# Attention output on TensorE: 64 matmuls of 32 rows and 32 columns a batch, or 40 of two shapes

## The chip, the cores and the metric

The kernel runs on one core of a Trainium2 chip. The metric is device time in microseconds (us) of one execution. The time before is 591.05 us, the median of three runs (589.9, 591.05 and 591.2).

## What is computed

A graph attention layer over 16 batches of 512 rows with 512 features, in fp32. Cut to what matters here:

```python
self_feat = concat([v, q], -1) @ W_self.T + b_self          # 16 x 512 x 512
output = self_feat
for d in range(2):                                          # both directions of the adjacency
    kv = self_feat[:, :20]                                  # 20 rows are keys and values
    aff = einsum('bnhd,bmhd->bnhm', qh, kh) / sqrt(32)      # 16 heads of 32
    w = softmax(where(mask, aff, NEG) + label_bias, -1)     # 20 weights a row, head, direction
    out_t = einsum('bnhm,bmf->bnhf', w, kv)
    output += einsum('bnhf,hgf->bnhg', out_t, Wout[d]) + bout[d]
return v + relu(output)
```

For each row and head there are 40 softmax weights, 20 of each direction. The kernel multiplies `kv` by `Wout` once, ahead of the loop, so that the attention output of a head is one product: its 40 weights by 40 value rows of 32 columns.

## The kernel before

**Setup** (to about 92 us): values, keys and bias terms of all batches are computed with small matmuls and written to DRAM. Line 544, 594, 658 and 683 are its matmuls; those of `keys` (L683) take 32 rows of the array and all 128 columns ("32\*128" in the profile's rows), those of L594 and L658 128 rows and 32 columns.

**Main loop**: 16 batches `b`, four tiles `nt` of 128 rows each. The instruction order is written out by hand, in program order for each engine. For a tile, TensorE computes `scores` (L357, 128 rows by 64 columns of the array, 32 records a tile); VectorE adds mask and bias terms, takes the maximum and subtracts it (`weigh`, L370, L374, L378); ScalarE takes the exponential (L383); in the next tile's step VectorE sums (L409) and takes the reciprocal (L410), GpSimd multiplies (`normal`, L411), and VectorE turns the weights (`turn`, L418). Between the scores TensorE computes the next batch's `self_feat` by seven half-size products (`product`, L284), which VectorE collects (`partial` L291, `joined` L301).

**The weights' place.** After `weigh` the partitions of a tile hold two head halves of 64 rows each; along a partition lie two row halves `g`, 8 heads, 2 directions and 20 weights: 640 numbers. `turn` is one VectorE transpose of 128x640, which turns each 32x32 block by itself. Afterwards a quarter `q` of the partitions holds 32 consecutive weights in its 32 rows, and 32 rows of the batch along the partition. As a head has 40 weights and a block 32, a head's weights lie in two neighbouring blocks.

**The values' place.** `blocks` (L152, 12 DMAs) writes the value rows to a DRAM tensor `bd_d`, after `clear_blocks` (L145) has filled all its 2 MB with zeros: for each head two blocks of 32 rows and 32 columns, the value rows at the places where the head's weights lie in the two blocks, and zeros elsewhere. `load_values` (L136, four DMAs a batch) loads a batch's blocks. All of these are issued from SyncE's queue (SP).

**The attention output.** `attend` (L420) runs over two column halves `c`, the two blocks `i`, four heads `e` and four quarters `q`: 64 matmuls, each 32 rows by 32 columns of the array, over 256 columns of moving data (4 tiles, 2 row halves, 32 rows). Quarter `q` picks the array's rows and the PSUM bank, `e` its columns; so 16 consecutive matmuls use 16 different parts of the array. Block `i=0` starts a sum in PSUM and `i=1` ends it. Each fp32 matmul is two passes, and each pass has a weight load of its own: a matmul leaves two load and two matmul records, 128 of each a batch. `attend(b - 1)` stands in tile `nt == 2` of batch `b`, after the scores of tile 1 and before those of tile 2; `finish` (L442) then adds `self_feat` on VectorE. The last batch is different: its scores, softmax, `turn_half` (L402, transposes of 128x320) and two calls of `attend` (three tiles, then one) stand at the end of the kernel, with `put_self` (L790) ahead of each.

Of the kernel before, what the change touches and what calls it, by code (L numbers as in the profile page):

```python
# [7 lines left out]
F32 = mybir.dt.float32  # L8
# [5 lines left out]
P = 128  # L14
# [4 lines left out]
def gat_kernel(  # L19
# [20 lines left out]
    nc = tc.nc  # L40
    B, F, N = xT.shape
    NG, L = adj.shape[3], adj.shape[4]
    H, DH = 16, 32
    C = F // P
    HL = P // DH
    NT = N // P
    BM = B * NG
    S = 2 * NG
    W = H * S
# [3 lines left out]
    HA = 2  # L53
    RA = P // HA
    HH = H // HA
    WA = WD // HA
    HN = (N - NG) // 2
    SCALE = float(1.0 / DH**0.5)

    PSUM = bass.MemoryType.PSUM  # L60
    DRAM = bass.MemoryType.DRAM
    const = ctx.enter_context(tc.tile_pool(name="const", bufs=1))
    dram = ctx.enter_context(tc.tile_pool(name="dram", bufs=1, space=DRAM))
# [6 lines left out]
    def bank(name, at=None):  # L70

        tag = {} if at is None else {"bufs": 1}
        return acc["pool"].tile([P, 512], F32, tag="acc" if at is None else f"acc{at}", name=name, **tag)
# [8 lines left out]
    bb_sb = const.tile([P, 1], F32, name="bb_sb")  # L82
    kvn = const.tile([P, C, BM], F32, name="kvn")
    g0 = const.tile([P, C, WD], F32, name="g0")
    zero = const.tile([P, HL * 2 * DH], F32, name="zero")

    cq_d = dram.tile([B, H, 2, NG], F32, name="cq_d")
    vw_d = dram.tile([2, C, BM, P], F32, name="vw_d")
    bd_d = dram.tile([C, B, 32, HL, 2, DH], F32, name="bd_d")
    g_d = dram.tile([C * C, P, B - 2, WD // C], F32, name="g_d")  # L90
    g1_d = dram.tile([C * C, P, WD // C], F32, name="g1_d")
    nz_d = dram.tile([B, N], F32, name="nz_d")
# [1 line left out]
    xs, xns, rss, adjs, nzs, sfs, cqs, gs, vds = {}, {}, {}, {}, {}, {}, {}, {}, {}  # L94
    adds, fulls, wts, outs, held, sf_ps, conds, prods = {}, {}, {}, [], [None] * 3, {}, {}, {}
# [39 lines left out]

    def load_values(b):  # L136

        vds[b] = gp.tile([P, HA, HL, 2, DH], F32, tag="vd", name=f"vd{b}", bufs=1)
        for q in range(HL):
            nc.sync.dma_start(  # L140
                vds[b][bass.ts(q, 32)].rearrange("p c e i g -> p c (e i g)"),
                bd_d[bass.ts(q // HA, HA), b].rearrange("c r e i g -> r c (e i g)"),
            )

    def clear_blocks(zero):  # L145

        nc.sync.dma_start(
            bd_d.rearrange("c b r e i g -> (c b r) (e i g)").rearrange("(n p) w -> p n w", p=P),
            zero.unsqueeze(1).to_broadcast([P, C * B * 32 // P, HL * 2 * DH]),
        )  # L150

    def blocks():  # L152

        bb = bd_d.rearrange("c b r e i g -> (c b) r e i g")
        vv = vw_d.rearrange("d c (b m) (e g) -> d (c b) m e g", m=NG, e=HL)
        for e in range(HL):
            for i in range(2):
                j = (e * S) // 32 + i
                for d in range(2):
                    lo = max(e * S + d * NG, 32 * j)  # L160
                    hi = min(e * S + (d + 1) * NG, 32 * j + 32)
                    if lo < hi:
                        m, r = lo - e * S - d * NG, lo - 32 * j
                        nc.sync.dma_start(bb[:, r : r + hi - lo, e, i], vv[d, :, m : m + hi - lo, e])


    def row_sum(b, j):
# [66 lines left out]
    def half(l):  # L234
        return slice(NG + l * HN, NG + (l + 1) * HN)

# [3 lines left out]
    def x_sum(b, n):  # L240

        t = sums[b, n] = xsum.tile([P, 2, HN], F32, tag=f"t{n}", name=f"t{b}_{n}")
        one, two = {
# [7 lines left out]
    def product(b, n):  # L251
# [17 lines left out]
        for i in range(2):  # L269
            for k in range(2):  # L270
                for a in range(HA):
# [5 lines left out]
                    if n in (2, 3, 5):  # L277
                        to = parts[b, "d" if n == 2 else "c"][bass.ts(a, RA), bass.ts(i, HN)]
                        start = k == 0 if n == 2 else (n, i, k) == (5, 0, 0)
                        stop = k == 1 if n == 2 else (n, i, k) == (3, 1, 1)  # L280
                    else:
                        to = parts[b, "a"][i][bass.ts(a, RA), :HN]
                        start, stop = (n, k) == (1, 0), (n, k) == (4, 1)
                    nc.tensor.matmul(to, lhs, x[:, k], start=start, stop=stop, skip_group_check=n != 2)  # L284

    def partial(b, n, f, l, to=None):

        if to is None:
            to = us[b, n] = xsum.tile([P, 2, HN], F32, tag=f"u{n}", name=f"u{b}_{n}")
        for i in range(2):  # L290
            done["partial"] = nc.vector.scalar_tensor_tensor(  # L291
                to[:, i], nzs[b][:, half(l)], qw[:, 2 * f + i, b : b + 1], parts[b, "a"][i][:, :HN],
                ALU.mult, ALU.add,
            )
# [72 lines left out]
    def weigh(b, nt, ps, between=None):  # L367

        f = softmax_view(fulls.pop((b, nt)))
        nc.vector.tensor_add(  # L370
            f[:, :, :, 1:], ps[:, :, :WA].rearrange("p g (h m) -> p g h m", m=ND), f[:, :, :, 1:]
        )
        mx = ps[:, 0, WA : WA + 2 * H].rearrange("p (g h) -> p g h", g=2)
        nc.vector.tensor_reduce(mx, f, AX.X, ALU.max)  # L374
        if between is not None:
            between()
        s = soft.tile(full, F32, tag="s", name=f"s{b}_{nt}", bufs=3)
        nc.vector.tensor_sub(s, f, mx.unsqueeze(3).to_broadcast(full))  # L378
        return s
# [16 lines left out]
    def normal_half(b, nt, s, a, engine):  # L396
# [2 lines left out]
        nc.vector.reciprocal(sm, sm)  # L399
        engine.tensor_mul(s[:, a], s[:, a], sm.unsqueeze(2).to_broadcast([P, H, NG]))  # L400

    def turn_half(b, nt, s, a):  # L402
        nc.vector.transpose(
            wts[b][:, nt, bass.ts(a, W // 2)], s[:, a].rearrange("p h m -> p (h m)")
        )

    def normal(b, nt, s):
        sm = soft.tile([P, 2, H], F32, tag="sm", name=f"sm{b}_{nt}")
# [4 lines left out]
    def turn(b, nt, s):  # L413


        if nt == 0:
            wts[b] = work.tile([P, NT, W], F32, tag="wt", name=f"wt{b}")
        nc.vector.transpose(wts[b][:, nt], s.rearrange("p a h m -> p (a h m)"))  # L418

    def attend(b, banks, tiles=slice(0, NT), start=True, stop=True):  # L420


        wt = wts[b][:, tiles].rearrange("p t (g w) -> p (t g) w", g=HA)
        w = wt.shape[1] * 32
        for c in range(HA):
            for i in range(2):
                for e in range(HL):
                    j = (c * HL + e) * S // 32 + i
                    for q in range(HL):
                        r = bass.ts(q, 32)  # L430
                        nc.tensor.matmul(  # L431
                            banks[q][bass.ts(e, DH), bass.ts(c, w)].rearrange("p (t n) -> p t n", n=32),
                            vds[b][r, c, e, i], wt[r, :, bass.ts(j, 32)],
                            start=start and i == 0, stop=stop and i == 1, skip_group_check=True,
                        )

    def turned(t, q, c=slice(0, HA), lo=0, hi=NT):

# [25 lines left out]
    with tc.tile_pool(name="setup", bufs=1) as sp, tc.tile_pool(name="ps_acc", bufs=4, space=PSUM) as acc["pool"]:  # L464
# [18 lines left out]
        with tc.tile_pool(name="setup_k", bufs=1) as sk:  # L483
# [81 lines left out]
            for c in range(C):  # L565
                nc.tensor.matmul(
                    ps[:, c % 2, c // 2 * B : (c // 2 + 1) * B], q4[:, bass.ts(c, P)], sel,
                    start=True, stop=True,
# [55 lines left out]
        with tc.tile_pool(name="setup_g", bufs=4) as sg:  # L624
# [49 lines left out]
            def keys(runs):  # L674
# [14 lines left out]
                for fc, hg, d, lo, hi in runs:  # L689
# [51 lines left out]
            first = None  # L741
            for n, runs in enumerate(bursts):
# [34 lines left out]
    gp = ctx.enter_context(tc.tile_pool(name="gp", bufs=2))  # L777
# [5 lines left out]
    with tc.manual_schedule():  # L783
# [13 lines left out]
        banks = None  # L797
        for b in range(B):
# [7 lines left out]
            for nt in range(NT):  # L806
# [20 lines left out]
                s = None  # L827

                if nt == 0:
# [41 lines left out]
                if nt == 1:  # L871
# [17 lines left out]
                    s = weigh(b, nt, pair)  # L889
# [10 lines left out]
                if nt == 2:  # L900
# [4 lines left out]
                    if b > 0:  # L905
                        banks = [bank(f"ps_o{b - 1}_{q}", q) for q in range(4)]
# [12 lines left out]
                    s = weigh(b, nt, pair, (lambda: partial(b + 1, 1, 0, 0)) if more else None)  # L919
# [10 lines left out]
                if nt == 3 and more:  # L930
# [18 lines left out]
                    s = weigh(b, nt, pair, lambda: partial(b + 1, 3, 1, 1))  # L949
# [9 lines left out]
                if final:  # L959
# [10 lines left out]
                    s = soft.tile(full, F32, tag="s", name=f"s{b}_{nt}", bufs=3)  # L970
# [11 lines left out]
        b = B - 1  # L982
# [23 lines left out]
        for q in (2, 3):  # L1006
            w = (NT - 1) * P
# [58 lines left out]
```

## Time and profile before

| | |
|---|---|
| runs | 589.9, 591.05, 591.2 us |
| the profiled execution | 591.14 us, of which 589.4 us are the span from the first to the last instruction |
| granted TensorE clock | 0.998 |
| TensorE matmul busy | 581.0 us (99%) |
| VectorE busy | 493.6 us (84%) |
| GpSimd busy | 382.6 us (65%) |
| ScalarE busy | 296.4 us (50%) |
| `attend`, matmuls of 256 columns, 15 batches | 41.4 us |

How to read it: a row of instructions gives the line of the kernel, the engine, the operation, the tile written and the tile read, the shapes, a count, and busy time and mean duration of one, or in views by time the start and the length in us. PE is TensorE's matmul, PEld its weight load, DVE VectorE, ACT ScalarE, POOL GpSimd, SP SyncE. "32\*32" in a matmul's row is the number of rows and columns of the array that it uses. Rows that touch are merged with a count; "<-" names what ended an idle time.

### The profile page before, as it was taken

How to read it: one execution, taken by the hardware profiler on the slowest of the kernel's cores; microseconds unless marked ns; L12 is line 12 of the kernel's file. 1: busy time of each engine (PE TensorE's matmuls, PEld its weight loads, DVE VectorE, ACT ScalarE, POOL GpSimd, SP SyncE). 2: the span in 40 equal slices, each digit the busy share in tenths (PEclk: the TensorE clock that was granted, in tenths of full speed). 3: DMA queues.
4: the chain of work that ended last, by engine and by line, in shares of the span. 5: the costliest groups of instructions: out<-in, count | busy, mean ns of one | idle time of the engine just before them, and what ended most of it. 6: DMA issues, size and time to landing. Idle time of an engine off the chain costs nothing.

```text
span 589.4 us, 17257 instructions
## 1 busy us (share of the span) xinstructions
PE 581.0 (99%) x7004; PEld 357.1 (61%) x7004; DVE 493.6 (84%) x785; ACT 296.4 (50%) x778; POOL 382.6 (65%) x351
## 2 busy tenths in 40 slices
PE   8999999999999999999999999999999999999996
PEld 4444447886666666666565656566666666666655
DVE  0496565889898989999898989898989898989896
ACT  1234442546464655556464646464747464646441
POOL 2225663648677675858585868685858586776774
PEclk9999999999999999999999999999999999999999
DMA  8999999966758495858675757666675757482504
GB/s 291 351 389 352 340 377 324 274 167 192 221 144 249 149 249 159 246 136 245 159 230 174 212 170 211 197 183 204 183 218 174 221 165 232 142 246 83 175 20 145
DMA packets 99615, 126.70 MB, mean 215 GB/s; under 512 B 19441, under 2 KB 71697, under 8 KB 97489
## 3 DMA queue, kind: packets, MB, share of 16 engines
q1 hardware_dynamic: 98288, 123.72, 68.3%
q0 software_dynamic: 672, 1.36, 1.0%
q8 instruction: 55, 0.90, 0.6%
q10 hardware_dynamic: 576, 0.53, 0.3%
q14 instruction: 24, 0.19, 0.1%
HBM read 85.71 MB, written 40.24 MB: 214 GB/s over the span
## 4 chain that ended last, share of the span: by engine, by line
PE 95%; DVE 2%; DMA 2%; ACT 0%; POOL 0%; SPq 0%; issue 0%; DVEq 0%; POOLq 0%; ACTq 0%
PE ps_s L357 44%; PE ps_a L284 17%; PE ps_c L284 8%; PE ps_o L431 7%; PE ps_d L284 4%; PE ps_v L658 3%; PE ps_k L594 3%; PE ps_sf L207 2%; DMA ws_q<-in_wsT 2%; PE ps_kv L544 1%; PE ps_nz L191 0%; POOL s L411 0%; PE ps_c L630 0%; PE ps_q L554 0%; PE ps_g(0, 2, 0, 1, 2)0_487 L683 0%
## 5 line engine op out<-in xcount | busy, mean ns | idle before, releaser
L357 PE MATMUL ps_s<-g,sf 128*64 128x304 f32 x2048 | 273.6, 420 | 0.5 <-ACT st L698 0.5
L357 PEld LDWEIGHTS ps_s<-g,sf 128*64 128x64 f32 x2048 | 152.2, 137 | 107.3 <-issue 6.2
L411 POOL TENSOR_TENSOR s<-s,sm 128x640 f32<-128x640 f32 x63 | 80.1, 1272 | 128.8 <-DVE sm L410 128.8
L383 ACT ACTIVATE s<-s 128x640 f32<-128x640 f32 x63 | 46.5, 738 | 167.4 <-DVE s L378 167.4
L319 ACT ACTIVATE prod<-adj,wb_sb 128x80 f32<-128x80 int32 x330 | 111.6, 427 | 0.0
L347 POOL TENSOR_TENSOR full<-cq,both 128x640 f32<-128x640 f32 x64 | 99.4, 1553 | 3.1 <-ACT both L338 1.5
L370 DVE TENSOR_TENSOR full<-ps_s,full 128x608 f32<-128x608 f32 x63 | 49.8, 791 | 36.1 <-PE ps_s L357 30.8
L455 POOL TENSOR_TENSOR o<-o,x 128x512 f32<-128x512 f32 x60 | 75.4, 1276 | 0.0
L338 ACT COPY both<-add 64x80 f32<-64x80 f32 x128 | 32.8, 256 | 51.1 <-DVE add L330 49.7
L284 PE MATMUL ps_a<-t,ws_s 128*64 128x246 f32 x480 | 55.1, 370 | 0.0
L374 DVE TENSOR_REDUCE ps_s<-full 128x32 f32<-128x640 f32 x63 | 52.2, 828 | 2.2
L409 DVE TENSOR_REDUCE sm<-s 128x32 f32<-128x640 f32 x63 | 50.8, 806 | 2.6 <-ACT s L383 0.9
L418 DVE STREAM_TRANSPOSE wt<-s 128x640 f32<-128x640 f32 x63 | 52.7, 837 | 0.1
L378 DVE TENSOR_TENSOR s<-full,ps_s 128x640 f32<-128x640 f32 x63 | 51.5, 818 | 1.1
L431 PE MATMUL ps_o<-wt,vd 32*32 32x256 f32 (+2 forms) x2176 | 45.2, 373 | 0.3 <-DVE wt L418 0.2
L284 PEld LDWEIGHTS ps_a<-t,ws_s 128*64 128x64 f32 x480 | 35.4, 137 | 15.9
L330 DVE TENSOR_REDUCE add<-prod 128x80 f32<-128x960 f32 x32 | 36.8, 1150 | 5.9 <-ACT prod L319 3.8
L249 POOL TENSOR_TENSOR t<-x 128x492 f32<-128x492 f32 x30 | 34.4, 1146 | 9.1 <-DVE full L370 4.6
L431 PEld LDWEIGHTS ps_o<-wt,vd 32*32 32x32 f32 x2176 | 30.1, 103 | 15.1 <-issue 7.0
L450 ACT ACTIVATE o<-o,bo 128x512 f32<-128x512 f32 x60 | 38.2, 707 | 1.2 <-POOL biased L898 1.2
L446 DVE TENSOR_TENSOR o<-ps_o,sf 128x512 f32<-128x512 f32 x60 | 36.7, 668 | 0.0
L291 DVE SCALAR_TENSOR_TENSOR u<-nz,qw,ps_a 128x246 f32<-128x246 f32 x90 | 36.6, 448 | 0.0
(238 smaller groups left out, 749.7 us busy)
## 6 DMA issues: line engine op xcount, KB each, us to landing
g_d<-st SPq DMA_DIRECT2D x16, 1064.0 KB, 6.3
g<-g_d SPq DMA_DIRECT2D x28, 608.0 KB, 4.9
out_T<-o SPq DMA_DIRECT2D x60, 256.0 KB, 4.8
xn<-in_xn SPq DMA_DIRECT2D x28, 512.0 KB, 3.7
x<-in_xT SPq DMA_DIRECT2D x28, 512.0 KB, 4.5
adj<-in_adj SPq DMA_DIRECT2D x32, 440.0 KB, 4.6
vd<-bd_d SPq DMA_DIRECT2D x64, 64.0 KB, 4.1
nz<-nz_d SPq DMA_DIRECT2D x14, 256.0 KB, 3.5
```

What stands on the lines that cost most here:

```text
L284: nc.tensor.matmul(to, lhs, x[:, k], start=start, stop=stop, skip_group_check=n != 2)
L319: nc.scalar.activation(p[:, :, l], a[:, :, l], AF.Identity, scale=wb_sb[:, l : l + 1])
L347: nc.gpsimd.tensor_add(f, cqs[b].unsqueeze(1).to_broadcast(shape), adds[b, nt // 2][:, nt % 2].unsqueeze(2).to_broadcast(shape),)
L357: nc.tensor.matmul(bank[bass.ts(a, RA), :WA], sfs[b][:, k, bass.ds(nt * P + g * RA, RA)], keys[:, k, a], start=(k == 0), stop=(k == C - 1),)
L370: nc.vector.tensor_add(f[:, :, :, 1:], ps[:, :, :WA].rearrange("p g (h m) -> p g h m", m=ND), f[:, :, :, 1:])
L374: nc.vector.tensor_reduce(mx, f, AX.X, ALU.max)
L378: nc.vector.tensor_sub(s, f, mx.unsqueeze(3).to_broadcast(full))
L409: nc.vector.tensor_reduce(sm, s, AX.X, ALU.add)
L411: done["normal"] = nc.gpsimd.tensor_mul(s, s, sm.unsqueeze(3).to_broadcast(full))
L418: nc.vector.transpose(wts[b][:, nt], s.rearrange("p a h m -> p (a h m)"))
L431: nc.tensor.matmul(banks[q][bass.ts(e, DH), bass.ts(c, w)].rearrange("p (t n) -> p t n", n=32), vds[b][r, c, e, i], wt[r, :, bass.ts(j, 32 ...
L455: nc.gpsimd.tensor_add(o[:, c], o[:, c], xs[b][:, c])
```

## The change

The first 16 weights of a head and direction, 32 a head, get a block of their own; the last 4 of each direction, 8 a head, of four heads share a fifth block. The turned weights of a tile are laid out as 16 blocks of the first kind (4/5 of the width) and 4 of the second. For that, `turn` becomes two VectorE transposes (128x512 and 128x128, whose sources are 16 and 4 of every 20 numbers), and `turn_half` two of half that size. `bd_d` holds per batch and column half a block of 32 rows by 128 columns for each kind: in the first, every column group of 32 has the rows of its own head; in the second, the rows of head `e` stand at rows 8`e` to 8`e`+7 in column group `e`, and the rest is zero. So only the second half of `bd_d` is cleared (1 MB), and `blocks` issues 10 DMAs (two with 16-row pieces of 512 bytes, eight with 4-row pieces of 128 bytes). `attend` issues for each column half first four matmuls of 32 rows and 128 columns (one a quarter, all four heads at once, starting the sum), and then 16 of 32 by 32 (ending it), with the quarter in the outer loop.

```diff
 def clear_blocks(zero):
-        bd_d.rearrange("c b r e i g -> (c b r) (e i g)").rearrange("(n p) w -> p n w", p=P),
+        bd_d[:, :, :, 1].rearrange("c b r w -> (c b r) w").rearrange("(n p) w -> p n w", p=P),
 def blocks():
-    for e in range(HL):
-        for i in range(2):
-            ...
-                    nc.sync.dma_start(bb[:, r : r + hi - lo, e, i], vv[d, :, m : m + hi - lo, e])
+    for d in range(2):
+        nc.sync.dma_start(bb[:, bass.ts(d, MW), 0], vv[d, :, :MW])
+    for e in range(HL):
+        for d in range(2):
+            at, w = e * 2 * RW + d * RW, bass.ts(e, DH)
+            nc.sync.dma_start(bb[:, at : at + RW, 1, w], vv[d, :, MW:, w])
+def turned_in(b, nt, s, g=slice(0, HA)):
+    n = s[:, g].shape[1]
+    f = s[:, g].rearrange("p g x m -> p (g x) m")
+    g0 = g.start
+    nc.vector.transpose(wts[b][:, nt, g0 * HH * 32 : (g0 + n) * HH * 32], f[:, :, :MW])
+    at = W * 4 // 5 + g0 * HA * 32
+    nc.vector.transpose(wts[b][:, nt, at : at + n * HA * 32], f[:, :, MW:])
 def turn_half(b, nt, s, a):
-    nc.vector.transpose(
-        wts[b][:, nt, bass.ts(a, W // 2)], s[:, a].rearrange("p h m -> p (h m)")
-    )
+    turned_in(b, nt, s, slice(a, a + 1))
 def turn(b, nt, s):
-    nc.vector.transpose(wts[b][:, nt], s.rearrange("p a h m -> p (a h m)"))
+    turned_in(b, nt, s)
 def attend(b, banks, tiles=slice(0, NT), start=True, stop=True):
-    for c in range(HA):
-        for i in range(2):
-            for e in range(HL):
-                j = (c * HL + e) * S // 32 + i
-                for q in range(HL):
-                    r = bass.ts(q, 32)
-                    nc.tensor.matmul(
-                        banks[q][bass.ts(e, DH), bass.ts(c, w)].rearrange("p (t n) -> p t n", n=32),
-                        vds[b][r, c, e, i], wt[r, :, bass.ts(j, 32)],
-                        start=start and i == 0, stop=stop and i == 1, skip_group_check=True,
-                    )
+    heads = wts[b][:, tiles, : W * 4 // 5].rearrange("p t (g j n) -> p t g j n", g=HA, n=32)
+    ends = wts[b][:, tiles, W * 4 // 5 :].rearrange("p t (g j n) -> p t g j n", g=HA, n=32)
+    ...
+    for c in range(HA):
+        for q in range(HL):
+            r = bass.ts(q, 32)
+            mm(q, c, slice(0, P), vds[b][r, c, 1], ends[r, :, :, c], True)
+        for q in range(HL):
+            r = bass.ts(q, 32)
+            for e in range(HL):
+                mm(q, c, bass.ts(e, DH), vds[b][r, c, 0, bass.ts(e, DH)], heads[r, :, :, c * HL + e], False)
```

More of the change, by code (lines that the diff above doesn't have):

```diff
@@ L57, in gat_kernel @@
     HN = (N - NG) // 2
+    MW = 16
+    RW = NG - MW
     SCALE = float(1.0 / DH**0.5)
@@ L84, in gat_kernel @@
     g0 = const.tile([P, C, WD], F32, name="g0")
-    zero = const.tile([P, HL * 2 * DH], F32, name="zero")
+    zero = const.tile([P, P], F32, name="zero")
     cq_d = dram.tile([B, H, 2, NG], F32, name="cq_d")
     vw_d = dram.tile([2, C, BM, P], F32, name="vw_d")
-    bd_d = dram.tile([C, B, 32, HL, 2, DH], F32, name="bd_d")
+    bd_d = dram.tile([C, B, 32, 2, P], F32, name="bd_d")
     g_d = dram.tile([C * C, P, B - 2, WD // C], F32, name="g_d")
@@ L136, in load_values @@
     def load_values(b):
-        vds[b] = gp.tile([P, HA, HL, 2, DH], F32, tag="vd", name=f"vd{b}", bufs=1)
+        vds[b] = gp.tile([P, HA, 2, P], F32, tag="vd", name=f"vd{b}", bufs=1)
         for q in range(HL):
             nc.sync.dma_start(
-                vds[b][bass.ts(q, 32)].rearrange("p c e i g -> p c (e i g)"),
-                bd_d[bass.ts(q // HA, HA), b].rearrange("c r e i g -> r c (e i g)"),
+                vds[b][bass.ts(q, 32)].rearrange("p c i w -> p c (i w)"),
+                bd_d[bass.ts(q // HA, HA), b].rearrange("c r i w -> r c (i w)"),
             )
@@ L147, in clear_blocks @@
         nc.sync.dma_start(
-            bd_d.rearrange("c b r e i g -> (c b r) (e i g)").rearrange("(n p) w -> p n w", p=P),
-            zero.unsqueeze(1).to_broadcast([P, C * B * 32 // P, HL * 2 * DH]),
+            bd_d[:, :, :, 1].rearrange("c b r w -> (c b r) w").rearrange("(n p) w -> p n w", p=P),
+            zero.unsqueeze(1).to_broadcast([P, C * B * 32 // P, P]),
         )
     def blocks():
-        bb = bd_d.rearrange("c b r e i g -> (c b) r e i g")
-        vv = vw_d.rearrange("d c (b m) (e g) -> d (c b) m e g", m=NG, e=HL)
+        bb = bd_d.rearrange("c b r i w -> (c b) r i w")
+        vv = vw_d.rearrange("d c (b m) w -> d (c b) m w", m=NG)
+        for d in range(2):
+            nc.sync.dma_start(bb[:, bass.ts(d, MW), 0], vv[d, :, :MW])
         for e in range(HL):
-            for i in range(2):
[L158 to L164, printed above, removed]
+            for d in range(2):
+                at, w = e * 2 * RW + d * RW, bass.ts(e, DH)
+                nc.sync.dma_start(bb[:, at : at + RW, 1, w], vv[d, :, MW:, w])
     def row_sum(b, j):
@@ L417, in turn, with mm @@
             wts[b] = work.tile([P, NT, W], F32, tag="wt", name=f"wt{b}")
-        nc.vector.transpose(wts[b][:, nt], s.rearrange("p a h m -> p (a h m)"))
+        turned_in(b, nt, s)
     def attend(b, banks, tiles=slice(0, NT), start=True, stop=True):
-        wt = wts[b][:, tiles].rearrange("p t (g w) -> p (t g) w", g=HA)
-        w = wt.shape[1] * 32
-        for c in range(HA):
-            for i in range(2):
-                for e in range(HL):
-                    j = (c * HL + e) * S // 32 + i
-                    for q in range(HL):
-                        r = bass.ts(q, 32)
-                        nc.tensor.matmul(
-                            banks[q][bass.ts(e, DH), bass.ts(c, w)].rearrange("p (t n) -> p t n", n=32),
-                            vds[b][r, c, e, i], wt[r, :, bass.ts(j, 32)],
-                            start=start and i == 0, stop=stop and i == 1, skip_group_check=True,
-                        )
+        n = tiles.stop - tiles.start
+        w = n * HA * 32
+        heads = wts[b][:, tiles, : W * 4 // 5].rearrange("p t (g j n) -> p t g j n", g=HA, n=32)
+        ends = wts[b][:, tiles, W * 4 // 5 :].rearrange("p t (g j n) -> p t g j n", g=HA, n=32)
+        def mm(q, c, to, lhs, rhs, first):
+            nc.tensor.matmul(
+                banks[q][to, bass.ts(c, w)].rearrange("p (t g n) -> p t g n", g=HA, n=32), lhs, rhs,
+                start=start and first, stop=stop and not first, skip_group_check=True,
+            )
+        for c in range(HA):
+            for q in range(HL):
[3 more added lines that the diff above has]
+                r = bass.ts(q, 32)
+                for e in range(HL):
+                    mm(q, c, bass.ts(e, DH), vds[b][r, c, 0, bass.ts(e, DH)], heads[r, :, :, c * HL + e], False)
     def turned(t, q, c=slice(0, HA), lo=0, hi=NT):
```

## Prediction

> **What bounds the kernel now.** I read the page first: the span and the shares, then the chain that ended last.
>
> ```profile
> span 589.4 us, 17257 instructions
> PE 581.0 (99%) x7004; PEld 357.1 (61%) x7004; DVE 493.6 (84%) x785; ACT 296.4 (50%) x778; POOL 382.6 (65%) x351
> PE 95%; DVE 2%; DMA 2%; ACT 0%; POOL 0%; SPq 0%; issue 0%; DVEq 0%; POOLq 0%; ACTq 0%
> ```
>
> TensorE is busy 99% of the span and carries 95% of the chain. A stretch of one batch in the loop shows the same with the others' reserves:
>
> ```profile
> 204.85:235.70 30.85, 30.85 (x372) 18.94 (x368) 28.07 (x44) 17.32 (x48) 21.88 (x20) 1.00 0.70 196
> ```
>
> The columns are the stretch, its length, and busy time of PE, PEld, DVE, ACT and POOL. TensorE has no gap in 30.85 us, at clock 1.00; VectorE is free for 30.85 - 28.07 = 2.78 us. So what counts is the time that `attend` keeps TensorE, 15 times in the loop, and whether VectorE keeps up.
>
> **Where `attend`'s time goes.** Busy time says little here, since 16 parts of the array work at once. The timeline of one `attend`, first TensorE's matmuls around its start and end, then its weight loads in short windows:
>
> ```profile
> 132.09 0.42 PE L357 MATMUL ps_s<-g,sf 128*64 128x304 f32 x1
> 132.44 0.50 PE L431 MATMUL ps_o<-wt,vd 32*32 32x256 f32 x16
> ```
>
> ```profile
> 132.44 0.23 PEld L431 LDWEIGHTS ps_o<-wt,vd 32*32 32x32 f32 x32 [0.46 <-issue]
> 133.09 0.36 PEld L431 LDWEIGHTS ps_o<-wt,vd 32*32 32x32 f32 x31
> 133.74 0.37 PEld L431 LDWEIGHTS ps_o<-wt,vd 32*32 32x32 f32 x31
> 134.39 0.33 PEld L431 LDWEIGHTS ps_o<-wt,vd 32*32 32x32 f32 x26
> 135.13 0.20 PEld L357 LDWEIGHTS ps_s<-g,sf 128*64 128x64 f32 x4 [0.41 <-issue]
> ```
>
> The loads come in four bursts, at 132.44, 133.09, 133.74 and 134.39, and the scores follow at 135.13: `attend` is 2.69 us, three rounds of 0.65 and a last one of 0.74. A round is 16 matmuls, each on its own part of the array, in two passes. What a pass costs is read from `keys` in the setup, whose matmuls have the shape that the change adds:
>
> ```profile
> 30.43 0.40 PE L683 MATMUL ps_g(0, 0, 1, 1, 2)0_403<-khD,wq_sb 32*128 32x152 f32 x2
> 30.45 0.40 PE L683 MATMUL ps_g(0, 0, 1, 1, 2)1_404<-khD,wq_sb 32*128 32x152 f32 x2
> 30.67 0.29 PE L683 MATMUL ps_g(0, 0, 1, 1, 2)0_403<-khD,wq_sb 32*128 32x152 f32 x2
> 30.80 0.42 PE L683 MATMUL ps_g(0, 0, 1, 1, 2)0_403<-khD,wq_sb 32*128 32x304 f32 x2
> 31.05 0.42 PE L683 MATMUL ps_g(0, 0, 1, 1, 2)0_403<-khD,wq_sb 32*128 32x304 f32 x2
> 31.07 0.42 PE L683 MATMUL ps_g(0, 0, 1, 1, 2)1_404<-khD,wq_sb 32*128 32x304 f32 x2
> 31.42 2.36 PE L594 MATMUL ps_k<-kvT,wk 128*32 128x320 f32 x32
> ```
>
> - A pass of 152 columns takes 30.80 - 30.67 = 0.13 us and one of 304 columns 31.05 - 30.80 = 0.25, 0.83 ns a column: 0.21 us for 256.
> - The first pass, 30.43 to 30.67, takes 0.24, not 0.13: a weight load of 128 columns that nothing covers costs 0.11 us.
> - The four quarters start within 0.02 us (30.43 and 30.45, 31.05 and 31.07).
> - The next shape starts at 31.42, 0.10 after the last pass has streamed (31.07 + 0.25); at 132.44 it is 132.09 + 0.25 + 0.10 as well. I take 0.09 to 0.10 for emptying the array at a change of shape.
>
> For the small matmuls the longest and the median record say what an uncovered load costs:
>
> ```profile
> L431 PE MATMUL ps_o<-wt,vd x2176: 211/375/400, 132.4 to 584.0; 32*32 32x256 f32 x175, 32*32 32x192 f32 x12, 32*32 32x64 f32 x11
> ```
>
> 400 - 375 = 25 ns. Two passes of 0.21 and this load make 0.45, yet a round takes 0.65. Its second pass starts at 132.44 + 0.03 + 0.21 = 132.68 and its first record ends 0.375 later, at 133.06; the next round's loads start at 133.09, when the first matmul of 16 has left, and not when its part of the array is free. I read this as 64 places for instructions: 16 matmuls of four instructions fill them, and the 17th has to wait. In the first case above, with 8 matmuls in all, the pass of 304 columns follows with no gap (30.67 + 0.13). The Trainium skill ("TensorE: Matmul & The Clock Gate", section "Architectural detail: the array is 16× 32×32, not 1× 128×128") gives TensorE a queue of 64; by that rule too the rounds here wait for places, and the trace agrees with its 0.65 us.
>
> **The change on TensorE.** It removes 24 of 64 matmuls, but no pass: 32 rows by 128 columns for four quarters fill the array as 16 small ones do, so there are still eight passes of 0.21 us a batch. What changes is that each round of 16 is now a shape of its own, and the array empties between. Does it empty where only the columns of the shape change? In the setup it does:
>
> ```profile
> 56.42 1.12 PE L191 MATMUL ps_nz<-rx,ones 128*128 128x512 f32 x2
> 57.48 0.42 PE L207 MATMUL ps_sf<-x,ws_v 128*64 128x236 f32 x2
> ```
>
> The next shape starts 0.06 us before the record's end (56.42 + 1.12), as at 31.42 (0.07) and 132.44 (0.07); inside a shape it is 0.16 (30.67 + 0.29 against 30.80). So I count an emptying at each of the two shapes:
>
> - Round of the shared blocks: 0.11 + 2 x 0.21 + 0.02 + 0.09 = 0.64 us.
> - Round of the small ones: 16 starts spread over 0.10 (132.44 + 0.50, less a record of 0.40, is 132.54), so 0.10 + 0.03 + 2 x 0.21 + 0.09 = 0.64.
> - Two column halves: 4 x 0.64 = 2.57 with unrounded terms, 0.11 under the 2.69 of now.
>
> This is the best case. The start spread of 0.10 holds if all 16 stand ready when the array is empty. Later rounds bring 31 loads in 0.36 us, or 0.26 between the first and the last start with loads of 0.10: 8.4 ns a load, 17 ns a matmul against 6.7 in the first round. In the changed kernel the four shared matmuls still hold 16 of the 64 places when the array has emptied (their records end 0.07 later), so 12 small ones are ready and four come in afterwards at 17 ns: 0.02 us more a round, perhaps 0.04, and 0.01 for the second shared round. I take 2.63, between 2.57 and 2.66: a gain of 0.06 us a batch (0.03 to 0.11), 0.9 us in 15 batches (0.45 to 1.65).
>
> **The change on VectorE.** Two transposes for one, each tile:
>
> ```profile
> L418 DVE STREAM_TRANSPOSE wt<-s 128x640 f32<-128x640 f32 x63 | 52.7, 837 | 0.1
> L403 DVE STREAM_TRANSPOSE wt<-s 128x320 f32<-128x320 f32 x2 | 1.0, 508 | 0.0
> ```
>
> From 320 to 640 elements 329 ns, 1.03 ns an element and 179 ns fixed: 705 ns for 512 and 311 for 128, together 1016 for 837. The tile's reserves are in the chain of VectorE around `attend`, and in its waits for the scores:
>
> ```profile
> 241.11 0.79 DVE L370 TENSOR_TENSOR full<-ps_s,full 128x608 f32<-128x608 f32 x1 [0.74 <-PE ps_s L357]
> 250.19 0.79 DVE L370 TENSOR_TENSOR full<-ps_s,full 128x608 f32<-128x608 f32 x1 [0.25 <-PE ps_s L357]
> 256.02 0.79 DVE L370 TENSOR_TENSOR full<-ps_s,full 128x608 f32<-128x608 f32 x1 [0.89 <-PE ps_s L357]
> 258.44 0.84 DVE L418 STREAM_TRANSPOSE wt<-s 128x640 f32<-128x640 f32 x1
> 259.20 2.44 DVE L446 TENSOR_TENSOR o<-ps_o,sf 128x512 f32<-128x512 f32 x4
> 262.95 0.79 DVE L370 TENSOR_TENSOR full<-ps_s,full 128x608 f32<-128x608 f32 x1 [0.19 <-PE ps_s L357]
> 264.51 0.84 DVE L291 SCALAR_TENSOR_TENSOR u<-nz,qw,ps_a 128x246 f32<-128x246 f32 x2
> ```
>
> The operation behind the transpose starts 0.08 before its end (258.44 + 0.84 against 259.20), so the second one adds 0.18 - 0.08 = 0.10 us in a row of work, 0.18 at most by the durations. Sources of 4 in 20 numbers are not in this trace; at double the time an element they would add another 0.13. Nearest is the whole row, so I take 0.10, with 0.3 as the far end. VectorE waits for the scores 0.19 to 0.89 us a tile: each wait covers 0.10, the two long ones 0.3 as well, and behind the least one (262.95) TensorE's nearest need of VectorE is `product` 6, which overwrites what `partial` has read by 264.51 + 0.84 = 265.35:
>
> ```profile
> 265.98 0.58 PE L284 MATMUL ps_a<-t,ws_s 128*64 128x246 f32 x4
> ```
>
> 0.63 us are left there. Hence nothing in the loop, and 0.4 of 2.78 us a batch used up.
>
> **The end of the kernel** has no such cover. In the chain that ended last:
>
> ```profile
> 577.44 0.84 DVE wt L418
> 582.19 0.52 DVE wt L403
> 582.76 1.50 PE ps_o L431 x82
> ```
>
> The transposes at 577.44 and 582.19 cost 0.10 each; the half before it ends ahead of an exponential and is covered. The last `attend`, over 64 columns (0.05 us a pass), becomes four rounds of about 0.33 with a record's tail: 1.43 for 1.50, 0.07 gained. Together +0.13 us (0 to 0.4).
>
> **DMA.** The clear halves and `blocks` issues 10 for 12, on SP:
>
> ```profile
> 110.01 10.57 SPq L164 DMA_DIRECT2D bd_d<-vw_d  x12
> 124.03 1.75 SPq L140 DMA_DIRECT2D vd<-bd_d  x4
> ```
>
> What stands behind them on SP, the loads of values and of the next batch, can only come earlier, and the first `attend` (132.44) starts without a wait for them: nothing.
>
> **Sum.** The profiled execution took 591.14 us: 591.14 - 0.9 + 0.13 = 590.4, from 589.5 (-1.65) to 591.1 (-0.45 + 0.4). The median of the runs lies 0.09 under this execution, so the forecast is 590.3 us. A measurement of this kernel can tell about 0.2%, 1.2 us: the likeliest single finding is no difference.
>
> **Rivals.**
>
> 1. *The places don't fill while the array empties* (slower). Then each round of small ones costs what the last one does now, 0.74, and a shared one 0.67: 2 x 1.41 = 2.82, 0.13 more a batch, 593.2 us. It decides from a small round over 0.70 us. Against it: the round at 132.44 directly follows another shape and starts at 6.7 ns a matmul. For it: that shape before held fewer places. 0.13.
> 2. *Emptying comes on top of the rounds*, because the 0.65 has another cause than places: three more emptyings of 0.09 and two loads of 0.11 for 0.03 are 0.43 a batch, 597.7 us. The Trainium skill ("TensorEngine Tiling (Array Packing)", "Key Properties") says that a change of tiling mode drains TensorE, and by that rule alone the change loses; the trace shows the drain, but also what it replaces. 0.04.
> 3. *No emptying between the two shapes*, as both have 32 rows: eight passes of 0.21 (1.7) and some 0.3 around them, 2.0 for 2.69, 580.5 us. Against it stands 57.48, where the rows were the same too. 0.06.
> 4. *The count sets the price*: 24 matmuls at 17 ns are 0.4 us a batch, 585 us. Against: a round is 0.65, while its 16 issues take 0.26. The Trainium skill ("TensorEngine Tiling (Array Packing)", "Instruction Overhead") puts about 60 cycles on every matmul, which would point the same way. 0.03.
> 5. *VectorE becomes the bound*: 2.78 / 4 = 0.7 us more a tile, seven times my 0.10. 0.02.
>
> **How the numbers follow.** The forecast has 0.72. Of that, 0.22 lie beyond 1.2 us of gain (rounds at the best case) and 0.50 within. With rivals 3 and 4 faster is 0.31, same 0.50; slower is 0.19 (1, 2 and 5). The forecast's own range is 589.4 to 591.0. The range for 8 in 10 leaves out 2 to 5 (0.15), and reaches from 589.0, a lowest case with the spread of the runs below their median, to rival 1 at 593.2.
>
> **What would show it.** In the changed trace: 80 matmul and 80 load records a batch in four bursts of loads, about 0.64 to 0.68 us apart; 2.57 to 2.66 us from the first load to the scores' load; records of 32\*128 of about 0.48 and 0.375; transposes of about 705 and 311 ns; a batch period of about 30.79 for 30.85, TensorE still without gaps, VectorE at about 28.5. Wrong if bursts overlap (rival 3), if the small round is over 0.70 (rival 1), or if TensorE waits for VectorE (5).

## The result and the profile after

| | before | changed |
|---|---|---|
| median of 16 runs each, us | 590.37 | 589.48 |
| lowest and highest, us | 589.75, 591.79 | 588.76, 590.64 |
| profiled execution, us | 591.14 | 589.24 |
| span, us | 589.4 | 587.5 |

The ratio changed/before is 0.9982, with a 95% interval of 0.9975 to 0.9990: 0.18% less, 0.6 to 1.5 us. That is a small gain, just inside the 0.2% taken as the bound of what can be told; the loop's period, below, tells it better than the times.

The page of the changed kernel, its first lines and the shares of the chain:

```profile
span 587.5 us, 15688 instructions
PE 579.4 (99%) x6188; PEld 345.8 (59%) x6188; DVE 497.1 (85%) x850; ACT 296.7 (51%) x778; POOL 382.8 (65%) x351
PE 95%; DVE 2%; issue 1%; POOL 0%; ACT 0%; DVEq 0%; POOLq 0%
```

TensorE has 816 matmul records fewer and still carries 95% of the chain; VectorE has 65 instructions and 3.5 us more. The stretch of 30.85 us in the loop that was shown of before, with the same columns:

```profile
204.85:235.70 30.85, 30.85 (x324) 18.28 (x322) 28.39 (x48) 17.38 (x49) 21.93 (x20) 1.00 0.69 197
```

TensorE has no gap, so the time is still the sum of what TensorE is given. VectorE is busy 28.39 us for 28.07. The weight loads of the first `attend`, in short windows of the timeline (start, length, engine, line, shapes, count):

```profile
130.97 0.31 PEld L435 LDWEIGHTS ps_o<-wt,vd 32*128 32x128 f32 x8 [0.46 <-issue]
131.61 0.25 PEld L435 LDWEIGHTS ps_o<-wt,vd 32*32 32x32 f32 x32 [0.33 <-issue]
132.27 0.31 PEld L435 LDWEIGHTS ps_o<-wt,vd 32*128 32x128 f32 x8 [0.41 <-issue]
132.92 0.25 PEld L435 LDWEIGHTS ps_o<-wt,vd 32*32 32x32 f32 x32 [0.33 <-issue]
133.58 0.20 PEld L356 LDWEIGHTS ps_s<-g,sf 128*64 128x64 f32 x4 [0.41 <-issue]
```

Four bursts of 8, 32, 8 and 32 loads, and the scores' loads at 133.58: `attend` keeps TensorE for 133.58 - 130.97 = 2.61 us, in rounds of 0.645 (shared) and 0.66 (small), where it was 2.69. It is the same in all 15 batches of the loop, and the time from one `attend` to the next falls by as much, from 30.85 to 30.77 us. The groups of the transposes and of `attend`'s matmuls, by shape (count, then busy time and mean ns of one):

```profile
L406 DVE STREAM_TRANSPOSE wt<-s 128x512 f32<-128x512 f32 x63 | 44.4, 705 | 0.1
L408 DVE STREAM_TRANSPOSE wt<-s 128x128 f32<-128x128 f32 x63 | 17.0, 271 | 0.0
```

```profile
L435 PE MATMUL ps_o<-wt,vd 32*32 32x256 f32 x960 | 21.9, 386 | 0.0
L435 PE MATMUL ps_o<-wt,vd 32*128 32x256 f32 x240 | 21.4, 426 | 0.0
```

The two groups' busy times overlap and aren't `attend`'s time: that is the 2.61 between the bursts, times 15, 39.1 us.

The last steps, in the chain that ended last (start, length, engine, what is written, line):

```profile
574.77 0.71 DVE wt L406
575.49 0.19 DVE wt L408
...
579.59 0.07 DVE wt L406
579.65 0.30 issue
579.96 0.21 DVE wt L408
580.17 0.04 issue
580.21 1.52 PE ps_o L435 x66
```

Here the transposes lie on the path: 0.91 from the start of the full one to the next operation for 0.84 before, and 0.62 from 579.59 to TensorE's start at 580.21 for 0.57 (582.19 to 582.76). From the start of the loop's last `attend` to VectorE's last operation it is 20.94 us for 20.83. As that `attend` is itself 0.08 shorter, what follows it is 0.19 us longer.

**The sum by the traces**: 15 x -0.08 + 0.19 = -1.0 us. The medians differ by 0.89 and the ratio says 1.06. The two spans differ by 1.9, but 1.47 of that lies ahead of the first `attend` (132.44 and 130.97), and the first experiment shows that this isn't the change's.

### The profile page after: what moved, and what is told of

Its sections match the earlier page's. It is cut to its first block, busy times and chain, and to the rows that moved or that the text cites. A ratio compares the mean times of both kernels' runs of the same rounds, so it can differ in the third digit from the quotient of the medians.

```text
span 587.5 us, 15688 instructions
## 1 busy us (share of the span) xinstructions
PE 579.4 (99%) x6188; PEld 345.8 (59%) x6188; DVE 497.1 (85%) x850; ACT 296.7 (51%) x778; POOL 382.8 (65%) x351
## 4 chain that ended last, share of the span: by engine, by line
PE 95%; DVE 2%; issue 1%; POOL 0%; ACT 0%; DVEq 0%; POOLq 0%
PE ps_s L356 44%; PE ps_a L283 17%; PE ps_c L283 8%; PE ps_o L435 6%; PE ps_d L283 4%; PE ps_v L670 3%; PE ps_k L606 3%; PE ps_sf L206 2%; PE ps_kv L556 2%; PE ps_warm L514 1%; DVE o L458 0%; PE ps_nz L190 0%; DVE sm L415 0%; DVE wt L406 0%; POOL s L417 0%
## 5 line engine op out<-in xcount | busy, mean ns | idle before, releaser
L406 DVE STREAM_TRANSPOSE wt<-s 128x512 f32<-128x512 f32 (+1 forms) x65 | 45.3, 697 | 0.1
L435 PE MATMUL ps_o<-wt,vd 32*32 32x256 f32 (+4 forms) x1360 | 43.9, 382 | 0.5 <-DVE wt L408 0.5
L248 POOL TENSOR_TENSOR t<-x,t 128x492 f32<-128x492 f32 x30 | 34.3, 1144 | 1.2
```

Source lines behind the costliest of these rows:

```text
L248: nc.gpsimd.tensor_sub(t, one, two)
L435: nc.tensor.matmul(banks[q][to, bass.ts(c, w)].rearrange("p (t g n) -> p t g n", g=HA, n=32), lhs, rhs, start=start and first, stop=stop a ...
```

## Experiments

**Both kernels once more** (`before_again`, `after_again`; no edit).

> The kernel before, unchanged, profiled once more. Places theory and count theory alike: a batch period of 30.85 us and 2.69 us for attend. What it is for is the setup: the scores of the main loop (the run of 64 score records) start at 100.41 us in the first profile and at 98.94 us in that of the changed kernel. If this 1.47 us is chance in when the first loads land, this profile starts its loop anywhere from 98.5 to 100.5 us; if it comes with the change, at 100.4 again.

> The changed kernel, unchanged, profiled once more. Expected: period 30.77 us, attend 2.61 us. If the earlier start of the loop is chance, it starts anywhere from 98.5 to 100.5 us; if it belongs to the change, at 98.9 again.

One run each: 589.89 and 589.61 us. The first and the following loads around the first `attend`, of the kernel before:

```profile
131.25 2.27 PEld L431 LDWEIGHTS ps_o<-wt,vd 32*32 32x32 f32 x128 [0.47 <-issue]
133.93 0.20 PEld L357 LDWEIGHTS ps_s<-g,sf 128*64 128x64 f32 x4 [0.41 <-issue]
```

and of the changed one:

```profile
131.54 0.31 PEld L435 LDWEIGHTS ps_o<-wt,vd 32*128 32x128 f32 x8 [0.47 <-issue]
...
134.15 0.45 PEld L356 LDWEIGHTS ps_s<-g,sf 128*64 128x64 f32 x6 [0.41 <-issue]
```

2.68 and 2.61 us again, to 0.01. The start is at 131.25 for the kernel before, where the first profile had 132.44, and at 131.54 for the changed one: this time the kernel before is the earlier. Over all twelve profiles of this study it lies between 130.72 and 132.44. Nearly all of this spread arises early: from the first of the setup's last matmuls (`ps_v`, at 42.07 us before and 40.57 changed) to the first `attend` all twelve have 90.37 to 90.40 us, and the first DMA that the change touches is issued at 97 us or later. So the setup's 1.47 us aren't the change's, and two single profiles can't be compared by their spans here; the loop's period can.

**Half the matmuls, in one shape** (`wide_halves`). The kernel before, with 32 matmuls of 32 rows by 64 columns a batch: the eight passes stay, a round has 8 matmuls, and there is no change of shape inside. Each wide matmul takes the two value blocks of one head for the columns of two heads, so other products are summed.

```diff
-                for e in range(HL):
-                    j = (c * HL + e) * S // 32 + i
+                for e in range(HL // 2):
+                    j = (c * HL + 2 * e) * S // 32 + i
...
-                            banks[q][bass.ts(e, DH), bass.ts(c, w)].rearrange("p (t n) -> p t n", n=32),
-                            vds[b][r, c, e, i], wt[r, :, bass.ts(j, 32)],
+                            banks[q][bass.ts(e, 2 * DH), bass.ts(c, w)].rearrange("p (t n) -> p t n", n=32),
+                            vds[b][r, c, 2 * e].rearrange("p i g -> p (i g)"), wt[r, :, bass.ts(j, 32)],
```

> The kernel before with matmuls of 32 rows by 64 columns, two heads of the output at once: 32 matmuls a batch, in four rounds of eight, still eight passes over the whole array and one shape. It computes other products than the reference (each matmul takes the two value blocks of one head for two heads' columns), so only its time is of use. Places theory: a round is 32 instructions, two rounds fit in 64 places, no round waits: 8 x 0.21 + 0.05 + 0.05 + 0.09 = 1.9 us for 2.69, period 30.06 us, about 579 us, up to 582 if VectorE then holds TensorE up. Rival, each round of the array has a fixed dead time of 0.22 us: 2.6 us, no change. Rival, a price of 3.3 ns for each matmul (0.08 us for 24): 0.11 us a batch, 589 us.

Measured: 579.27 us for 590.66, ratio 0.9815 (0.9801 to 0.9829). Its loads, and a stretch of one period:

```profile
131.60 1.53 PEld L431 LDWEIGHTS ps_o<-wt,vd 32*64 32x64 f32 x64 [0.47 <-issue]
133.51 0.45 PEld L357 LDWEIGHTS ps_s<-g,sf 128*64 128x64 f32 x6 [0.38 <-issue]
```

```profile
204.85:234.92 30.07, 30.07 (x308) 18.45 (x306) 27.92 (x44) 17.32 (x48) 21.89 (x20) 1.00 0.72 201
```

133.51 - 131.60 = 1.91 us: eight passes of 0.21, and 0.2 for the first load and the emptying. The bursts have no gaps any more, one entry holds all 64 loads. So the 0.2 us that each round of 16 loses is no fixed cost of a round: with half the instructions in the same four rounds it is gone. Nor is it a price of each matmul: 32 matmuls fewer save 0.78 us here, 24 fewer saved 0.08 in the change. Of the theories above only the waiting for places gives both numbers.

Two more rivals fall by rows already shown. A price of each instruction that binds only where they are many would spread the loads evenly, but the kernel before loads from 133.09 to 133.45 and then pauses until 133.74. And a pause that matmuls of 32 columns need by themselves would show in the setup, where four of L594 stand side by side and no more: its row at 31.42 has eight passes of 320 columns in 2.36 us. Less the last record of 0.43, that leaves 1.93 for the seven steps from pass to pass, 0.28 each, where a pass of 304 columns took 0.25; so there is none. What no run varies is the number of places itself.

TensorE still has no gap at a period of 30.07, with VectorE at 27.92.

**The two transposes alone** (`split_turn`). The kernel before, each transpose cut in two of the change's sizes, from unbroken sources.

```diff
-        nc.vector.transpose(wts[b][:, nt], s.rearrange("p a h m -> p (a h m)"))
+        f = s.rearrange("p a h m -> p (a h m)")
+        nc.vector.transpose(wts[b][:, nt, : W * 4 // 5], f[:, : W * 4 // 5])
+        nc.vector.transpose(wts[b][:, nt, W * 4 // 5 :], f[:, W * 4 // 5 :])
```

> The kernel before with its transposes alone cut in two (128x512 and 128x128 from contiguous sources, halves likewise); attend untouched. My theory: VectorE's part costs nothing in the loop (period 30.85 us, VectorE at 28.4) and about 0.2 us at the end, 590.6 us. Rival, VectorE's second transpose is felt in the loop: 0.1 us in each of 60 tiles, 596 us.

Measured: 590.96 us for 590.63, ratio 1.0004 (0.9995 to 1.0014): nothing. Its groups and the end of its chain:

```profile
L420 DVE STREAM_TRANSPOSE wt<-s 128x512 f32<-128x512 f32 x63 | 44.4, 705 | 0.1
L421 DVE STREAM_TRANSPOSE wt<-s 128x128 f32<-128x128 f32 x63 | 17.0, 269 | 0.0
```

```profile
581.51 0.46 DVE wt L405
581.96 0.04 issue
582.01 1.50 PE ps_o L434 x81
```

705 and 269 ns, where the change's sources of 16 and of 4 in every 20 numbers take 705 and 271: reading in pieces costs nothing. The period is that of before (30.84 us), so the second transpose is hidden in the loop. At the end the expected 0.2 us did not come. TensorE starts at 582.01, 0.50 after the half transpose began and so before the second of the two was through: in this order the first matmuls need only the first piece. In the change they need the last one, as the shared blocks come first.

**One transpose with the new matmuls** (`one_turn`). The changed kernel with the transpose of before; the weights don't get their new places.

```diff
-        f = s[:, g].rearrange("p g x m -> p (g x) m")
-        g0 = g.start
-        nc.vector.transpose(wts[b][:, nt, g0 * HH * 32 : (g0 + n) * HH * 32], f[:, :, :MW])
-        at = W * 4 // 5 + g0 * HA * 32
-        nc.vector.transpose(wts[b][:, nt, at : at + n * HA * 32], f[:, :, MW:])
+        at = g.start * W // 2
+        nc.vector.transpose(
+            wts[b][:, nt, at : at + n * W // 2], s[:, g].rearrange("p g x m -> p (g x m)")
+        )
```

> The changed kernel with one transpose of 128x640 for the two (halves likewise), so that the weights stand where attend doesn't look for them: it leaves out the new order of the weights, and only its time is of use. My theory: loop unchanged (period 30.77 us, VectorE back at 28.07), 0.2 us less at the end, 589.2 us. Rival, VectorE holds part of the gain back in the loop: period under 30.77 us.

Measured: 589.28 us for 590.66, ratio 0.9984 (0.9974 to 0.9995), as the change. `attend` is 2.61 and the period 30.77 us; from the last `attend` of the loop to VectorE's last operation it is 20.81 us, 0.13 less than in the change. So the loop's gain is TensorE's alone, and the transposes cost 0.13 us, all at the end.

**The quarter in the inner loop** (`quarter_inner`). The changed kernel, with the small matmuls in the order of before.

```diff
-            for q in range(HL):
-                r = bass.ts(q, 32)
-                for e in range(HL):
+            for e in range(HL):
+                for q in range(HL):
+                    r = bass.ts(q, 32)
```

> The changed kernel with the head in the outer and the quarter in the inner loop of the small matmuls, as before the change. Places theory: each small matmul has its own part of the array in either order, so 2.61 us and no difference (below 0.2%). Rival, the order by quarters is part of the gain: up to 0.08 us a batch lost, 1.2 us.

Measured: 589.41 us for 590.66, ratio 0.9983 (0.9973 to 0.9994); `attend` 133.52 - 130.91 = 2.61 us:

```profile
130.91 0.31 PEld L435 LDWEIGHTS ps_o<-wt,vd 32*128 32x128 f32 x8 [0.47 <-issue]
...
133.52 0.45 PEld L356 LDWEIGHTS ps_s<-g,sf 128*64 128x64 f32 x6 [0.41 <-issue]
```

In the loop the order in a round makes no difference (period 30.77 us). At the end it does, a little: from the loop's last `attend` to VectorE's last operation it is 21.03 us, 0.09 more than in the change, as VectorE's last additions begin later.

**The shared rounds together** (`shared_first`). In the changed kernel both halves' shared matmuls come first, then both halves' small ones: two changes of shape fewer, no other work. (This kernel leaves out the shared sums of the first column half: the second half's start flag sets the whole PSUM bank to be overwritten. The Trainium skill, "PSUM — Partial Sum Buffer", section "The four PSUM rules", gives the 2 KiB bank as the reach of that flag; no time here shows it.)

```diff
         for c in range(HA):
             for q in range(HL):
                 r = bass.ts(q, 32)
                 mm(q, c, slice(0, P), vds[b][r, c, 1], ends[r, :, :, c], True)
+        for c in range(HA):
             for q in range(HL):
```

> Same 40 matmuls, but all eight shared ones first and then all 32 small ones: two changes of shape fewer a batch. Places theory: shared part 0.11 + 4 x 0.21 + 0.02 + 0.09 = 1.07 us, small part a waiting round of 0.65 and a last one of 0.74, together 2.46 us, 0.15 under the changed kernel: period 30.62 us, about 2.2 us less in 15 batches, 587.2 us. Count theory (a price for each matmul): 40 matmuls as before the edit, 2.61 us, no difference to the changed kernel.

Measured: 588.11 us for 590.63, ratio 0.9945 (0.9930 to 0.9961). Its loads:

```profile
131.20 0.74 PEld L435 LDWEIGHTS ps_o<-wt,vd 32*128 32x128 f32 x16 [0.47 <-issue]
132.27 1.01 PEld L435 LDWEIGHTS ps_o<-wt,vd 32*32 32x32 f32 x64 [0.33 <-issue]
133.70 2.25 PEld L356 LDWEIGHTS ps_s<-g,sf 128*64 128x64 f32 x20 [0.41 <-issue]
```

`attend` takes 2.50 us and the period is 30.66. The two shared rounds take 1.07 (132.27 - 131.20) where they were 2 x 0.645 = 1.29. The 0.21 saved (before rounding) is near to the uncovered load and the emptying (0.11 and 0.09) that the prediction put on a change of shape. The two small rounds take 1.43 where they were 2 x 0.66: now the second stands directly behind the first, and waits for places; 1.39 had been expected. So a change of shape has a use too: while the array empties, the queue fills.

15 x 0.19 are 2.8 us; the medians differ by 2.5 and the ratio says 3.2. The profiled execution, 588.74 us, is the slowest of the six: from the loop's last `attend` to VectorE's last operation it has 22.19 us, 1.25 more than the change. VectorE's and GpSimd's operations there, and TensorE after them:

```profile
577.66 1.33 DVE L399 TENSOR_TENSOR s<-s,sm 128x320 f32<-128x320 f32 x1
577.65 0.99 POOL L1026 TENSOR_TENSOR o<-o,x 128x384 f32<-128x384 f32 x1 [0.61 <-ACT o L1021]
579.65 2.15 PE L435 MATMUL ps_o<-wt,vd 32*128 32x64 f32 x80 [1.25 <-DVE wt L408]
```

VectorE's multiply takes 1.33 us, as against 0.49 in the change, while GpSimd's add runs. That is 0.84 us; the last `attend` is slow too, 2.15 us at a lower clock, as the last section shows. The next two runs show whether these belong to the new order.

**The same with all sums kept** (`shared_first_kept`): only the first half's matmuls carry the start flag.

```diff
-                start=start and first, stop=stop and not first, skip_group_check=True,
+                start=start and first and c == 0, stop=stop and not first, skip_group_check=True,
```

> As shared_first, but only the first column half's shared matmuls carry the flag that starts a sum in a PSUM bank; in shared_first the second half's start took the first half's shared sums with it. The flag costs no time: attend 2.50 us, period 30.66 us, 588.1 us as in shared_first, and again VectorE's multiply at the end at 1.3 us beside GpSimd's add (0.49 us in the changed kernel). If that collision was chance, 0.5 to 1.2 us less at the end.

Measured: 587.91 us for 590.86, ratio 0.9955 (0.9941 to 0.9970); `attend` 2.50, period 30.66. From the loop's last `attend` to VectorE's last operation it is 20.64 us, 1.55 less than in `shared_first`, where 0.5 to 1.2 had been expected: 0.84 is the multiply, and 0.69 the last `attend`, which takes 1.46 us for 2.15. This time the multiply takes 0.49 and GpSimd's add 1.35:

```profile
577.58 0.49 DVE L399 TENSOR_TENSOR s<-s,sm 128x320 f32<-128x320 f32 x1
577.57 1.35 POOL L1026 TENSOR_TENSOR o<-o,x 128x384 f32<-128x384 f32 x1 [0.61 <-ACT o L1021]
```

**And the short transpose first** (`short_turn_first`): as `shared_first_kept`, with the two transposes of `turned_in` in the other order, so that the shared blocks, which `attend` needs first, are turned first.

> As shared_first_kept, but the short of the two transposes goes first in each tile, since the shared matmuls that read its result go first on TensorE. My theory of the end: the last attend waits for both transposes only because the one it needs comes second; with the short one first its shared matmuls start about 0.3 us earlier beside the long transpose: 20.3 us from the loop's last attend to VectorE's last operation, for 20.64. Rival, VectorE's work at the end sets the time whatever the order: 20.6 again. In the loop nothing either way, period 30.66 us; about 587.6 us, 0.3 us being too little for the times to tell.

Measured: 588.55 us for 590.36, ratio 0.9967 (0.9954 to 0.9980). The step itself does what it should: at the end TensorE starts 0.30 us after the first transpose has begun, and doesn't wait for the second. But from the loop's last `attend` to VectorE's last operation it is 21.17 us, not 20.3, as the multiply ahead of the transposes takes 1.33 again; without those 0.84 us it would be 20.33:

```profile
578.29 1.33 DVE L399 TENSOR_TENSOR s<-s,sm 128x320 f32<-128x320 f32 x1
579.65 0.24 DVE L407 STREAM_TRANSPOSE wt<-s 128x64 f32<-128x64 f32 x1
579.82 0.40 DVE L408 STREAM_TRANSPOSE wt<-s 128x256 f32<-128x256 f32 x1
```

```profile
579.95 1.46 PE L435 MATMUL ps_o<-wt,vd 32*128 32x64 f32 x80 [1.21 <-DVE wt L407]
```

In these three profiles the two operations begin within 0.01 us of each other, and one of them takes longer: VectorE's by 0.84, or GpSimd's by 0.36 (1.35 for 0.99). In the other nine profiles it is GpSimd's. The Trainium skill ("SBUF — State Buffer", "SBUF: two separate sides") says that VectorE, in an operation with two inputs in SBUF such as this one, and GpSimd share a port that the first to start holds for its whole instruction. The trace agrees in that one of the two always takes longer; who started first it doesn't tell, as GpSimd's row begins 0.01 us ahead in all three. The new order itself isn't the cause, as `shared_first_kept` has it too. What decides between the two outcomes is not shown; it is worth 0.84 us at the end.

**Shared rounds together in the loop only** (`shared_first_loop`): the grouped order where `attend` starts the sums, the change's order in the last call, and the start flag as in `shared_first_kept`.

```diff
-        for c in range(HA):
+        for cs in ((0, 1),) if start else ((0,), (1,)):
+            for c in cs:
+                ...
+                    mm(q, c, slice(0, P), vds[b][r, c, 1], ends[r, :, :, c], True)
+            for c in cs:
+                ...
+                        mm(q, c, bass.ts(e, DH), vds[b][r, c, 0, bass.ts(e, DH)], heads[r, :, :, c * HL + e], False)
```

> Shared matmuls of both column halves first in the 15 batches of the loop only; the two calls at the end in the order of the changed kernel. Places theory with the collision at the end caused by the order there: attend 2.50 us in the loop, period 30.66 us, the end as in the changed kernel (20.83 us from the last attend of the loop to VectorE's last operation, for 20.94): 0.11 x 15 = 1.6 us under the changed kernel, 587.9 us, 0.45% under the kernel before. If the end is late whatever the order there, 589 us.

Measured: 587.68 us for 590.86, ratio 0.9949 (0.9935 to 0.9963). Its median is the lowest of the kernels that form all the sums, though the 0.2 us to `shared_first_kept` are within the spread of the runs. It is 3.2 us under the kernel before. Under the change it is 1.8 by the medians, whose kernels before differ by 0.5 themselves, and 15 x 0.11 = 1.6 by the period of 30.66. The end takes 20.83 us, as expected. Its loads:

```profile
131.82 0.74 PEld L435 LDWEIGHTS ps_o<-wt,vd 32*128 32x128 f32 x16 [0.47 <-issue]
132.90 0.56 PEld L435 LDWEIGHTS ps_o<-wt,vd 32*32 32x32 f32 x34 [0.33 <-issue]
133.55 0.37 PEld L435 LDWEIGHTS ps_o<-wt,vd 32*32 32x32 f32 x30
134.32 0.20 PEld L356 LDWEIGHTS ps_s<-g,sf 128*64 128x64 f32 x4 [0.41 <-issue]
```

Two shared rounds of 16 loads pass without a gap; the second small round begins at 133.55, 0.65 after the first, as the rounds of before did, and its loads spread over 0.37 us, where the 32 of a round that stands ready in the changed kernel take 0.25.

## Why the prediction was right

The mechanism held. The time itself came out near the edge of the forecast's range: 589.48 us for 590.3 (589.4 to 591.0). Most of that, 0.68 us, is the time of before, 591.05 as the median of three runs and 590.37 of sixteen; the change from it was forecast as -0.77 and measured as -0.89. The likeliest finding, no difference on a scale of 0.2%, came out by little: it is 0.18%. The terms point by point:

- **The places.** A round of 16 small matmuls waits for room for their instructions. `wide_halves` decides it: with 8 in a round the wait is gone. It also explains the size of the gain. The 24 removed matmuls are no passes, so they could only give back waiting, 0.2 us in each of three rounds, and the three new changes of shape take most of that: `attend` went from 2.69 to 2.61 us, the forecast was 2.63 and 2.57 to 2.66.
- **Emptying where only the columns change.** It happens, as 57.48 in the setup had suggested: the shared round is 0.645 (forecast 0.64). Rival 3, with no emptying, is out. `shared_first` gives the price of one such change, with its load, as 0.21 us.
- **The places fill while the array empties.** The loads of a small round take 0.25 us for 32, against 0.23 when the queue stood ready and 0.36 when it did not. Of 16 matmuls 14 start at 6.7 ns and the last two 13 and 16 ns behind the one before; I had taken 12 and four. The small round is 0.66 us, under the 0.70 from which rival 1 decides, and no more than my 0.64 with its 0.02. Rival 2's waits on top and rival 4's price for each matmul both fall with `wide_halves`.
- **VectorE.** 705 ns was exact, the short transpose takes 271 and not 311: the line through 320 and 640 elements doesn't hold for short ones (64 elements take 202 ns at the end, where it gives 245). The whole is 976 and not 1016 for 837. The stretch has 28.39 (forecast 28.5), and `split_turn` shows the loop's cost as nothing. The far end of 0.3, for sources in pieces, is excluded: 271 against 269.
- **The end** was mis-sized: +0.19 us, where I had +0.13. The transposes cost 0.13 in all (`one_turn`) and not 0.20. The last `attend` was wrong in sign: from TensorE's start to VectorE's last operation 0.07 lost for 0.07 gained. TensorE's own part of it is 0.02 to 0.03 (1.52 for 1.50 in the chains, 1.51 for 1.48 in the timelines); behind its end VectorE's last additions begin 0.04 later than before. Its bursts in the changed kernel:

```profile
580.21 0.31 PEld L435 LDWEIGHTS ps_o<-wt,vd 32*128 32x128 f32 x8 [0.44 <-DVE wt L408]
580.93 0.31 PEld L435 LDWEIGHTS ps_o<-wt,vd 32*128 32x128 f32 x8
581.31 0.25 PEld L435 LDWEIGHTS ps_o<-wt,vd 32*32 32x32 f32 x32
```

A shared round over 64 columns takes 581.31 - 580.93 = 0.38 us, and a shared and a small one 580.93 - 580.21 = 0.72, which leaves 0.34 for the small one; I had 0.33 for each. The loads of 128 columns run to 0.31 after the round's start, longer than two passes of 0.05: I take it that with so few columns the loads set a shared round, which my sum of passes and one load leaves out.

- **Setup and DMA**: nothing, as forecast; the 1.7 us within which the first `attend` starts arise ahead of anything that the change touches. After VectorE's last operation the profiles have between 4.2 and 5.2 us to their end: 4.24 in both of the kernel before, 4.82 and 4.62 in the two of the changed one. With 4.48 in `split_turn`, which has the old `attend`, and 4.28 in `shared_first` the two kinds meet; whether the rest is chance too stays open, and the sum by the traces leaves it out.

The forecast sum, -0.9 + 0.13 = -0.77, stands against -1.0 by the traces and -0.9 to -1.06 measured; the missing 0.2 is the 0.02 us a batch that `attend` was better, 0.3 in 15 batches, less the 0.06 by which the end was worse.

## What to carry to other kernels

Count what small matmuls hold in the queue, not only what they stream: where a round of them fills it, as 16 fp32 matmuls of four instructions do here, half as many wider ones for the same passes took 0.78 us off 2.69. Removing matmuls without removing passes gave back waiting only, and each change of shape, even in columns alone, took 0.1 to 0.2 us of it, so here it paid to put the rounds of the shape with the larger weight load next to each other. Where two kernels differ by 1 us in 590, compare a period in the loop and not the span of two profiles, whose setup alone differed by up to 1.7 us.

## What the runs showed of the hardware that was not expected

- A transpose on VectorE that reads 4 or 16 of every 20 numbers takes as long as one that reads them unbroken (271 and 705 against 269 and 705 ns).
- VectorE's 0.49 us multiply took 1.33 when GpSimd's add began 0.01 us ahead of it, and in another profile with the same 0.01 it did not: it was then GpSimd's that took longer (1.35 for 0.99).
- TensorE's clock fell after a short gap in one profile. `shared_first` and `short_turn_first` over their last `attend` (stretch, length, busy time of PE, PEld, DVE, ACT and POOL, then the granted clock, the DMA share and GB/s):

```profile
579.65:581.80 2.15, 2.15 (x80) 1.74 (x80) 0.94 (x3) 0.00 (x0) 0.20 (x1) 0.51 0.19 64
```

```profile
579.95:581.41 1.46, 1.46 (x80) 1.21 (x80) 1.28 (x4) 0.00 (x0) 0.52 (x1) 1.00 0.06 11
```

After 1.25 us without matmuls the one ran at 0.51, and after 1.21 us the other at 1.00. The clock records of the traces suggest what decides. In all twelve the full clock lasts a whole number of steps of 3.413 us (566.61 us are 166, 573.44 are 168, 576.85 are 169, 580.27 are 170). In `shared_first` it falls at 579.69, right behind the gap from 578.41 to 579.65. In `short_turn_first` the steps lie at 578.87, 0.12 us into the gap from 578.75 to 579.95, and at 582.28, where it falls, but behind the last matmul (581.41). So what counts may be how much of a gap lies within one step; no run varied that alone.
